# A selective scan that carries its state between chunks: GpSimd's additions to the first column against a first value read by the scan

## The chip, the core and the metric

The kernel runs on one core of a Trainium2 chip. The metric is the device time of one execution in microseconds, the median of several runs. All data are float32. The engines are PE (TensorE, matrix products), VectorE (DVE in the profile), ScalarE (ACT), GpSimd (POOL) and SyncE (SP), which issues nearly all DMAs.

## The reference

The program computes six layers on a tensor of 2 images of 64 x 64 positions with 128 channels: a convolutional selective scan (layer 0), a deformable convolution (layer 1), a selective scan (layer 2, first half), a spectral convolution (layer 2, second half), linear attention, and a mixture of experts. The change lies in the selective scan of layer 2:

```python
x_proj = x @ W_in
xs, z = jnp.split(x_proj, 2, axis=-1)
delta = xs @ W_delta
Bv = xs @ W_B
Cv = xs @ W_C
deltaA = jnp.exp(jnp.einsum('bld,dn->bldn', delta, A))
deltaB = jnp.einsum('bld,bln->bldn', delta, Bv)
def step(state, inp):
    dA_i, dB_i, x_i, C_i = inp
    state = dA_i * state + dB_i * x_i[:, None, :]
    y = jnp.einsum('bdn,bn->bd', state, C_i)
    return (state, y)
```

There are 2 images of 4096 tokens, 256 inner channels d and 256 state columns n. So for each image 256 x 256 first-order recurrences run over 4096 tokens.

## The kernel before, in words

`layer2` (L952 and following) runs the scan and, woven into it, the spectral convolution. Tokens are cut into chunks of T = 512: 8 chunks (c) for each of the 2 images (b), 16 chunks in all, in order. On the chip the 256 channels that the recurrence runs over independently are called d; the index n lies on the 128 partitions in two halves h.

For one chunk, d runs over 256 values, in 32 groups gi of DG = 8. Four values of d together are a row of work (R = 4); a chunk has 64 rows. For one row:

- SP loads `row` (L1306): delta for four d and 512 tokens, spread to all partitions (1 MB into SBUF). Three buffers; the load stands two rows ahead.
- GpSimd multiplies `row` by `g` into `S` (L1318), 128 x 4096 values: the inputs of the recurrences of four d and both halves. This stands one row ahead. `S` has three buffers of two rows.
- ScalarE makes `dA` = exp(delta x A) for one d and one h (L1374) into PSUM, three buffers.
- VectorE runs the recurrence over the 512 tokens of one d and one h in place in `S` (L1376, a scan: s[t] = dA[t] x s[t-1] + S[t]). Eight scans to a row.

After a group, `contract` lets PE multiply `S` with `cv` (L1336), ScalarE copies the product `ze` (L1342), and SP stores it.

Between the chunks of one image the last token's values must be carried over. ScalarE copies the last column of each group of `S` into the tile `state` (L1378), 128 partitions x 2 halves x 256 columns, in SBUF. In the next chunk of that image (c > 0) the kernel before forms the first step of the recurrence by hand. With delta of the first token, `scan_inputs` makes `ea` = exp(A x delta of the first token) (L909 to L914). GpSimd multiplies `state` by `ea`, most columns at d = 0 and the last 16 at d = 16 (L1323). After each multiplication L1318 it adds the decayed state to the first token's column of `S` (L1324, 128 x 8 values). The scan itself starts from the constant 0.

What goes beside the scan is written out by hand. `layer2` runs under a manual schedule: after each d the loop makes one step of each of several generators. These are `scan_inputs` for the next chunk (started at group 12 of 32), `outputs` for the chunk before, `contract`, and the spectral convolution (`convolve`, L1202, PE), which gets a share of steps by a credit. Each engine works its instructions in the order in which the loop records them. The inputs of the very first chunk are made during layer 1 by `first_inputs` and kept in DRAM.

Of the kernel before, what the change touches and what calls it, by code (L numbers as in the profile page):

```python
# [16 lines left out]
F32 = mybir.dt.float32  # L17
I32 = mybir.dt.int32
BF16 = mybir.dt.bfloat16
AF = mybir.ActivationFunctionType  # L20
ALU = mybir.AluOpType
# [4 lines left out]
P = 128  # L26
# [4 lines left out]
N = 512  # L31
# [835 lines left out]
    return (wdr, mdr), work  # L867


def scan_inputs(k, b, c, x1, rs, sh, w_in, a_t, sm, cst, gc, ddr, ps, got):  # L870

    nc, ins, T = k.nc, k.ins, N
    NB = T // P
    xi = sm.tile([P, NB, C], F32, name="xi", tag="s2")
    nc.sync.dma_start(out=xi, in_=x1[b * L + c * T : b * L + (c + 1) * T, :].rearrange("(i p) c -> p i c", p=P))
    for _ in range(4):
        yield
    pt = ps.tile([P, N], F32, name="pt", tag="ps")
    for j in range(NB):
        i = b * NTB + c * NB + j  # L880
        o = sm.tile([P, C], F32, name="xn", bufs=2)
        nc.scalar.activation(o, xi[:, j, :], AF.Identity, bias=sh[:, i : i + 1], scale=rs[:, i : i + 1])
        nc.tensor.transpose(pt[:, j * P : (j + 1) * P], o, k.ident)
        yield
    xt = sm.tile([P, T], F32, name="xt2", tag="s2")
    nc.scalar.copy(xt, pt)
    xtd = ddr.tile([P, T], F32, name="xtd")
    nc.sync.dma_start(out=xtd, in_=xt)
    yield
    xs = sm.tile([P, 2, N], F32, name="xs", tag="s4")  # L890
    for h in range(2):
        px = ps.tile([P, N], F32, name="px2", tag="ps")
        nc.tensor.matmul(px, w_in[:, h * P : (h + 1) * P], xt, start=True, stop=True)
        yield
        nc.scalar.copy(xs[:, h, :], px)
    ea = cst.tile([P, 2, 256], F32, name="ea")
    g = gc.tile([P, 2, T], F32, name="g")
    cv = gc.tile([P, 2, T], F32, name="cv")
    drow = ddr.tile([256, T], F32, name="drow")
    for w_, what in (("w_delta2", 0), ("w_b2", 1), ("w_c2", 2)):  # L900
        w = cst.tile([P, 2, 256], F32, name="w")
        nc.sync.dma_start(out=w, in_=ins[w_].rearrange("(a p) c -> p a c", p=P))
        yield
        yield
        if what == 0:

            pd = ps.tile([P, N], F32, name="pd0", tag="ps")
            for i in range(2):
                nc.tensor.matmul(pd[:, :256], xs[:, i, 0:1].to_broadcast([P, P]), w[:, i, :], start=i == 0, stop=i == 1)  # L909
            yield  # L910
            yield
            nc.vector.tensor_tensor(ea, a_t, pd[:, :256].unsqueeze(1).to_broadcast([P, 2, 256]), ALU.mult)
            yield
            nc.scalar.activation(ea, ea, AF.Exp)  # L914
        for h in range(2):
            pw = ps.tile([P, N], F32, name="pw2", tag="ps")
            for i in range(2):
                nc.tensor.matmul(pw, w[:, i, h * P : (h + 1) * P], xs[:, i, :], start=i == 0, stop=i == 1)
            yield
            yield  # L920
            if what == 0:
                d = sm.tile([P, N], F32, name="d", tag="s2")
                nc.scalar.copy(d, pw)
                nc.sync.dma_start(out=drow[h * P : (h + 1) * P, :], in_=d)
            elif what == 1:
                nc.vector.tensor_tensor(g[:, h, :], pw, xs[:, h, :], ALU.mult)
            else:
                nc.scalar.copy(cv[:, h, :], pw)
    got.append((xtd, g, cv, drow, ea))


def first_inputs(k, es, ps, dr, x1, rs, sh):

    nc = k.nc
    pool = es.enter_context(k.tc.tile_pool(name="l2e", bufs=1))
    w_in = pool.tile([P, 256], F32, name="w_in0")
    nc.sync.dma_start(out=w_in, in_=k.ins["w_in2"][:, :256])
    a_t = pool.tile([P, 2, 256], F32, name="a_t0")
    nc.sync.dma_start(out=a_t, in_=k.ins["a2"].rearrange("(a p) c -> p a c", p=P))
    got = []  # L940
    for _ in scan_inputs(k, 0, 0, x1, rs, sh, w_in, a_t, pool, pool, pool, dr, ps, got):
        pass
    xtd, g, cv, drow, ea = got[0]
    kept = []
    for t, name in ((g, "g0"), (cv, "cv0"), (ea, "ea0")):
        d = dr.tile(list(t.shape), F32, name=name)
        nc.sync.dma_start(out=d, in_=t)
        kept.append(d)
    return xtd, kept[0], kept[1], drow, kept[2]


def layer2(k, x1, x3, rs, sh, wdr, mdr, early):  # L952
# [13 lines left out]
    tc, nc, ins = k.tc, k.nc, k.ins  # L966
    T = N
    NB = T // P
    NCH = L // T
    DG = 8  # L970
    NG = 256 // DG
    R = 4
    HKW = 2 * (13 * P + DW)
    with ExitStack() as es:
# [34 lines left out]
            return x[t0 : t0 + T, :].rearrange("(i p) c -> p i c", p=P)  # L1009

        def prologue(b, c, got):
            return scan_inputs(k, b, c, x1, rs, sh, w_in, a_t, sm, cst, gc, ddr, ps, got)

        def epilogue(b, c, xtd, zd):

# [293 lines left out]
        def make_inputs(r):  # L1309
            i, r = divmod(r, 256 // R)  # L1310
            if i < len(todo):
                d = r * R
                gi, q = divmod(d, DG)
                if q == 0:
                    Ss[i, gi] = sp.tile([P, 2, DG, T], F32, name="S")
                S = Ss[i, gi][:, :, q : q + R, :]
                row, g, ea = rows[i, r], ready[i][1], ready[i][4]
                nc.gpsimd.tensor_tensor(S, row.unsqueeze(1).to_broadcast([P, 2, R, T]), g.unsqueeze(2).to_broadcast([P, 2, R, T]), ALU.mult)  # L1318
                if todo[i][1] > 0:
                    if d in (0, 2 * DG):  # L1320

                        m = slice(0, 256 - 2 * DG) if d == 0 else slice(256 - 2 * DG, 256)
                        nc.gpsimd.tensor_tensor(state[:, :, m], state[:, :, m], ea[:, :, m], ALU.mult)  # L1323
                    nc.gpsimd.tensor_tensor(S[:, :, :, 0], S[:, :, :, 0], state[:, :, d : d + R], ALU.add)  # L1324

        def contract(i, gi, zd):
            S, cv = Ss.pop((i, gi)), ready[i][2]
# [18 lines left out]

        with tc.manual_schedule():
            got = []
            xtd, g0, cv0, drow, ea0 = early
            g, cv, ea = gc.tile([P, 2, T], F32, name="g"), gc.tile([P, 2, T], F32, name="cv"), cst.tile([P, 2, 256], F32, name="ea")  # L1350
            for dst, src in ((g, g0), (cv, cv0), (ea, ea0)):
                nc.scalar.dma_start(out=dst, in_=src)
            ready[0] = xtd, g, cv, drow, ea
            for r in range(2):
                load_row(r)
            make_inputs(0)
            zq, save, credit = [], None, 0
            for i, (b, c) in enumerate(todo):
                _, g, cv, drow, ea = ready[i]
                zd = ddr.tile([NG, NB, P, 32, DG], F32, name="zd")  # L1360
                if i + 1 < len(todo):
                    pro = prologue(*todo[i + 1], got)
                for gi in range(NG):
                    for j in range(DG):
                        d = gi * DG + j
                        r = i * (256 // R) + d // R
                        if d % R == 0:
                            load_row(r + 2)
                            make_inputs(r + 1)
                        S = Ss[i, gi]  # L1370
                        row = rows[i, d // R]
                        for h in range(2):
                            dA = pa.tile([P, T], F32, name="dA2")
                            nc.scalar.activation(dA, row[:, j % R, :], AF.Exp, scale=a_t[:, h, d : d + 1])  # L1374
                            s = S[:, h, j, :]
                            nc.vector.tensor_tensor_scan(s, dA, s, 0.0, ALU.mult, ALU.add)  # L1376
                        if j == 2 and save is not None:
                            nc.scalar.copy(*save)  # L1378
                            save = None
                        advance(zq)  # L1380
                        if gi == 1 and j == 4 and i > 0:

                            side.append(outputs(*todo[i - 1], ready.pop(i - 1)[0], zd_))
                        if gi == 12 and j == 0 and i + 1 < len(todo):
                            side.append(pro)
                        step(side)
                        if got:
                            ready[i + 1] = got.pop()
                        now[0] += 1
                        credit = min(credit + 4.8, 4.8)  # L1390
                        credit -= spent[0]
                        spent[0] = 0
                        while credit > 0 and back:
                            credit -= step(back) or 4
                    if c < NCH - 1:
                        save = state[:, :, gi * DG : (gi + 1) * DG], S[:, :, :, T - 1]
                    zq.append(contract(i, gi, zd))
                zd_ = zd
# [367 lines left out]
```

## Time and profile before

| what | value |
|---|---|
| median of 3 runs | 15351.72 us (15348.02 to 15357.47) |
| the profiled execution's own time | 15384.23 us |
| its span, first to last instruction | 15382.4 us |
| layer 2's scans, first to last start | 5186.1 to 14882.6 us |
| busy: PE, DVE, ACT, POOL | 12387.6, 12707.2, 9497.0, 13019.5 us |
| L1324, GpSimd's addition to the first column | 896 times, 211 ns |
| L1323, GpSimd's decay of the state | 14 times 1212 ns, 14 times 257 ns |
| L912, VectorE, and L914, ScalarE, for `ea` | 16 times 660 ns, 16 times 630 ns |
| L1378, ScalarE's copy into `state` | 448 times, 202 ns |

The profile is one execution, so its times belong to that execution's 15384 us and not to the median. An engine's busy time counts its instructions, not its waits. A group of instructions is named by its line in the kernel, its engine, what it writes and reads, and its shape (partitions x elements). A wait is put down to the instruction that ended it. On VectorE the end of one instruction overlaps the start of the next in the records, so the distance between two starts says what an instruction costs there, and its duration says a little more.

### The profile page before, as it was taken

The page shows a single profiled execution, that of the slowest core. Times are in us where ns is not written, and L with a number is a line of the kernel's source. Part 1 is how long each engine was busy: PE and PEld are TensorE (multiplying, and loading weights), DVE is VectorE, ACT ScalarE, POOL GpSimd, SP SyncE. Part 2 cuts the span into 40 slices and gives each one's busy share as a digit, 9 for nine tenths or more (in the row PEclk, how much of TensorE's full clock was granted, in tenths as well). Part 3 has the DMA queues.
Part 4 walks back from the last instruction along what each step waited for, and adds up shares of the span by engine and source line. Part 5 has one row for each costly group of instructions (what it writes and reads, how often), then busy time and mean ns, then how long its engine had stood idle before and what let it go on. Part 6 is the DMA issues. An engine that isn't in the chain of part 4 may idle for free.

```text
span 15382.4 us, 234681 instructions
## 1 busy us (share of the span) xinstructions
PE 12387.6 (81%) x91214; PEld 7926.4 (52%) x91214; DVE 12707.2 (83%) x11405; ACT 9497.0 (62%) x14103; POOL 13019.5 (85%) x4168
## 2 busy tenths in 40 slices
PE   7888788888777545497896888978888899898897
PEld 4544454444577413254563555645445555555565
DVE  6777657777453799999999999999999999999973
ACT  4666436655001477777777677777777777777752
POOL 5888638888287899999999999999999999999960
PEclk8999899999888767698997999989999999999998
DMA  6888748888565445465555555555666666666543
GB/s 158 200 194 196 187 105 197 197 195 191 166 199 162 148 151 167 155 203 180 194 193 171 185 189 193 199 185 191 200 190 201 191 196 204 191 196 200 189 161 134
DMA packets 1444903, 2809.37 MB, mean 183 GB/s; under 512 B 393136, under 2 KB 1110608, under 8 KB 1240784
## 3 DMA queue, kind: packets, MB, share of 16 engines
q1 hardware_dynamic: 1395936, 2638.55, 58.3%
q0 software_dynamic: 46560, 153.18, 3.3%
q8 instruction: 721, 11.81, 0.3%
q14 instruction: 390, 3.19, 0.1%
q10 hardware_dynamic: 1296, 2.63, 0.0%
HBM read 2372.53 MB, written 421.31 MB: 182 GB/s over the span
## 4 chain that ended last, share of the span: by engine, by line
POOL 43%; PE 23%; DVE 12%; DMA 10%; issue 4%; ACT 3%; SPq 3%; another core or an unknown queue 1%; POOLq 0%; ACTq 0%; DVEq 0%
POOL S L1318 36%; DVE S L1376 9%; PE pef L1202 6%; DMA row<-drow 6%; POOL S L391 3%; PE Z L443 3%; PE Z L1336 2%; POOL G L742 2%; PE dA L411 2%; DMA W<-bcd 2%; PE acc L1175 2%; SPq L430 1%; DVE S L482 1%; PE pv L756 1%; PE pd L333 1%
## 5 line engine op out<-in xcount | busy, mean ns | idle before, releaser
L1376 DVE TENSOR_TENSOR_SCAN S<-dA,S 128x512 f32<-128x512 f32 x8192 | 9225.7, 1199 | 387.5 <-ACT dA L1374 204.1
L1318 POOL TENSOR_TENSOR S<-row,g 128x4096 f32<-128x4096 f32 x1024 | 9104.3, 8898 | 241.4 <-DMA row<-drow 159.7
L1374 ACT ACTIVATE dA<-row,a_t 128x512 f32<-128x512 f32 x8192 | 5614.6, 692 | 2165.9 <-DVE S L1376 2131.1
L1336 PE MATMUL Z<-S,cv 128*32 128x256 f32 x32768 | 2506.4, 436 | 1508.1 <-ACT ze L1342 1230.9
L1202 PE MATMUL pef<-hk,ur 128*128 128x256 f32 x14336 | 3514.1, 388 | 134.7 <-ACT e L1182 116.7
L1202 PEld LDWEIGHTS pef<-hk,ur 128*128 128x128 f32 x14336 | 2646.9, 191 | 1074.4 <-issue 564.1
L482 DVE TENSOR_TENSOR_SCAN S<-dA,S 128x1024 f32<-128x1024 f32 x1024 | 2309.3, 2283 | 758.6 <-ACT dA L425 422.8
L391 POOL TENSOR_TENSOR S<-row,bt 128x2048 f32<-128x2048 f32 x512 | 2383.8, 4656 | 432.8 <-PE Z L443 334.3
L1336 PEld LDWEIGHTS Z<-S,cv 128*32 128x32 f32 x32768 | 1003.4, 121 | 2718.1 <-issue 1229.5
L443 PE MATMUL Z<-S,W 128*32 128x128 f32 x16384 | 1191.5, 434 | 438.4 <-DMA W<-bcd 218.1
L1342 ACT COPY ze<-Z 128x512 f32<-128x512 f32 x1024 | 1122.4, 1096 | 232.5 <-PE Z L1336 196.2
L425 ACT ACTIVATE dA<-dA 128x1020 f32<-128x1020 f32 x1024 | 1028.6, 1010 | 378.0 <-PE dA L411 339.3
L411 PE MATMUL dA<-dt,quad 64*128 64x255 f32 x8192 | 1183.4, 414 | 19.8 <-DVE S L482 19.3
L443 PEld LDWEIGHTS Z<-S,W 128*32 128x32 f32 x16384 | 715.0, 170 | 818.3 <-issue 288.1
L1175 PE MATMUL acc<-e,mw 128*128 128x512 f32 x1920 | 1048.4, 634 | 29.6 <-ACT e L1182 28.8
L411 PEld LDWEIGHTS dA<-dt,quad 64*128 64x128 f32 x8192 | 750.9, 195 | 580.4 <-issue 385.3
L1202 PEld LDWEIGHTS pef<-hd,ur 128*128 128x128 f32 x4096 | 758.3, 194 | 493.7 <-issue 235.0
L742 POOL DMA_INDIRECT G<-table,idx x576 | 807.2, 1401 | 219.8 <-issue 167.9
L1202 PE MATMUL pef<-hd,ur 128*128 128x256 f32 (+1 forms) x4096 | 876.7, 340 | 102.0 <-ACT e L1182 95.5
L749 DVE TENSOR_TENSOR G<-G,wt 128x4608 f32<-128x4608 f32 x64 | 317.8, 4966 | 557.0 <-DMA G<-table,idx 537.2
L1182 ACT COPY e<-pef 128x512 f32<-128x512 f32 x960 | 557.9, 587 | 109.6 <-PE pef L1202 60.7
L756 PE MATMUL pv<-ident,G 128*128 128x128 f32 x4608 | 569.2, 285 | 30.0 <-issue 29.6
(341 smaller groups left out, 7858.9 us busy)
## 6 DMA issues: line engine op xcount, KB each, us to landing
row<-drow SPq DMA_DIRECT2D x1536, 1024.0 KB
zd<-ze SPq DMA_DIRECT2D x1024, 256.0 KB
hk<-in_phi_dram SPq DMA_DIRECT2D x128, 576.5 KB
hk<-in_phi_dram SPq DMA_DIRECT2D x96, 704.5 KB
hd<-in_phi_dram SPq DMA_DIRECT2D x512, 128.5 KB
mw<-wdr SPq DMA_DIRECT2D x480, 128.0 KB
hk<-in_phi_dram SPq DMA_DIRECT2D x160, 320.5 KB
hk<-in_phi_dram SPq DMA_DIRECT2D x96, 448.5 KB
```

The lines of the kernel that those rows point to most:

```text
L391: nc.gpsimd.tensor_tensor(S[:, o, :], rows.pop(s), bt[:, sub * T : (sub + 1) * T].unsqueeze(1).to_broadcast([P, 8, T]), ALU.mult)
L411: nc.tensor.matmul(dA[:, 2 * a + h, rest], stats[d, j][r, h, :], dt[r, h, at : at + T - 1], start=True, stop=True)
L443: nc.tensor.matmul(Z[32 * q : 32 * q + 32, :, :, a].rearrange("p t g -> p g t"), w, S[:, :, t : t + 13 : 4], start=True, stop=True)
L482: nc.vector.tensor_tensor_scan(flat, dflat, flat, 0.0, ALU.mult, ALU.add)
L742: nc.gpsimd.indirect_dma_start(out=G[:, o, :], out_offset=None, in_=table[b], in_offset=bass.IndirectOffsetOnAxis(ap=idxs[b][:, i * 9 + o ...
L1175: nc.tensor.matmul(acc.rearrange("p a s -> p (a s)"), ms[f][:, o, :], e, start=box["first"], stop="whole" in box and (f, o) == todo[-1])
L1202: nc.tensor.matmul(pe[:, a, 256 - n :], ur[:, par, j, :], h[:, at : at + n], start=i == 0, stop=i + 1 == len(mm))
L1318: nc.gpsimd.tensor_tensor(S, row.unsqueeze(1).to_broadcast([P, 2, R, T]), g.unsqueeze(2).to_broadcast([P, 2, R, T]), ALU.mult)
L1336: nc.tensor.matmul(Z[32 * j : 32 * j + 32, q], cv[:, h, s], S[:, h, :, s], start=h == 0, stop=h == 1)
L1342: nc.scalar.copy(ze.rearrange("p q t e -> p q e t"), Z)
L1374: nc.scalar.activation(dA, row[:, j % R, :], AF.Exp, scale=a_t[:, h, d : d + 1])
L1376: nc.vector.tensor_tensor_scan(s, dA, s, 0.0, ALU.mult, ALU.add)
```

## The change

Each scan of a chunk with c > 0 takes its first value from the column of `state` that belongs to its d and h, in place of the constant 0. With that, s[0] = dA[0] x state + S[0], and dA[0] is the same exponential that `ea` was. GpSimd's additions (L1324) and the decay of the state (L1323) go, and with them all that made `ea`: the two products, the multiplication and the exponential in `scan_inputs`, with three of the generator's steps, the load of `a2` into `a_t0`, and the store and load of `ea0` for the first chunk. ScalarE's copy into `state` stays as it is.

```diff
-def scan_inputs(k, b, c, x1, rs, sh, w_in, a_t, sm, cst, gc, ddr, ps, got):
+def scan_inputs(k, b, c, x1, rs, sh, w_in, sm, cst, gc, ddr, ps, got):
...
-    ea = cst.tile([P, 2, 256], F32, name="ea")
...
-        if what == 0:
-
-            pd = ps.tile([P, N], F32, name="pd0", tag="ps")
-            for i in range(2):
-                nc.tensor.matmul(pd[:, :256], xs[:, i, 0:1].to_broadcast([P, P]), w[:, i, :], start=i == 0, stop=i == 1)
-            yield
-            yield
-            nc.vector.tensor_tensor(ea, a_t, pd[:, :256].unsqueeze(1).to_broadcast([P, 2, 256]), ALU.mult)
-            yield
-            nc.scalar.activation(ea, ea, AF.Exp)
...
-    a_t = pool.tile([P, 2, 256], F32, name="a_t0")
-    nc.sync.dma_start(out=a_t, in_=k.ins["a2"].rearrange("(a p) c -> p a c", p=P))
...
-    for t, name in ((g, "g0"), (cv, "cv0"), (ea, "ea0")):
+    for t, name in ((g, "g0"), (cv, "cv0")):
...
-                row, g, ea = rows[i, r], ready[i][1], ready[i][4]
+                row, g = rows[i, r], ready[i][1]
                 nc.gpsimd.tensor_tensor(S, row.unsqueeze(1).to_broadcast([P, 2, R, T]), g.unsqueeze(2).to_broadcast([P, 2, R, T]), ALU.mult)
-                if todo[i][1] > 0:
-                    if d in (0, 2 * DG):
-
-                        m = slice(0, 256 - 2 * DG) if d == 0 else slice(256 - 2 * DG, 256)
-                        nc.gpsimd.tensor_tensor(state[:, :, m], state[:, :, m], ea[:, :, m], ALU.mult)
-                    nc.gpsimd.tensor_tensor(S[:, :, :, 0], S[:, :, :, 0], state[:, :, d : d + R], ALU.add)
...
-            for dst, src in ((g, g0), (cv, cv0), (ea, ea0)):
+            for dst, src in ((g, g0), (cv, cv0)):
                 nc.scalar.dma_start(out=dst, in_=src)
...
-                            nc.vector.tensor_tensor_scan(s, dA, s, 0.0, ALU.mult, ALU.add)
+                            nc.vector.tensor_tensor_scan(s, dA, s, state[:, h, d : d + 1] if c > 0 else 0.0, ALU.mult, ALU.add)
```

More of the change, by code (lines that the diff above doesn't have):

```diff
@@ L928, in scan_inputs @@
                 nc.scalar.copy(cv[:, h, :], pw)
-    got.append((xtd, g, cv, drow, ea))
+    got.append((xtd, g, cv, drow))
 def first_inputs(k, es, ps, dr, x1, rs, sh):
@@ L937, in first_inputs @@
     nc.sync.dma_start(out=w_in, in_=k.ins["w_in2"][:, :256])
-    a_t = pool.tile([P, 2, 256], F32, name="a_t0")
-    nc.sync.dma_start(out=a_t, in_=k.ins["a2"].rearrange("(a p) c -> p a c", p=P))
     got = []
-    for _ in scan_inputs(k, 0, 0, x1, rs, sh, w_in, a_t, pool, pool, pool, dr, ps, got):
+    for _ in scan_inputs(k, 0, 0, x1, rs, sh, w_in, pool, pool, pool, dr, ps, got):
         pass
-    xtd, g, cv, drow, ea = got[0]
+    xtd, g, cv, drow = got[0]
     kept = []
-    for t, name in ((g, "g0"), (cv, "cv0"), (ea, "ea0")):
+    for t, name in ((g, "g0"), (cv, "cv0")):
         d = dr.tile(list(t.shape), F32, name=name)
@@ L948, in first_inputs @@
         kept.append(d)
-    return xtd, kept[0], kept[1], drow, kept[2]
+    return xtd, kept[0], kept[1], drow
 def layer2(k, x1, x3, rs, sh, wdr, mdr, early):
@@ L1011, in prologue @@
         def prologue(b, c, got):
-            return scan_inputs(k, b, c, x1, rs, sh, w_in, a_t, sm, cst, gc, ddr, ps, got)
+            return scan_inputs(k, b, c, x1, rs, sh, w_in, sm, cst, gc, ddr, ps, got)
         def epilogue(b, c, xtd, zd):
@@ L1348, in layer2 @@
             got = []
-            xtd, g0, cv0, drow, ea0 = early
-            g, cv, ea = gc.tile([P, 2, T], F32, name="g"), gc.tile([P, 2, T], F32, name="cv"), cst.tile([P, 2, 256], F32, name="ea")
-            for dst, src in ((g, g0), (cv, cv0), (ea, ea0)):
+            xtd, g0, cv0, drow = early
+            g, cv = gc.tile([P, 2, T], F32, name="g"), gc.tile([P, 2, T], F32, name="cv")
+            for dst, src in ((g, g0), (cv, cv0)):
                 nc.scalar.dma_start(out=dst, in_=src)
-            ready[0] = xtd, g, cv, drow, ea
+            ready[0] = xtd, g, cv, drow
             for r in range(2):
@@ L1358, in layer2 @@
             for i, (b, c) in enumerate(todo):
-                _, g, cv, drow, ea = ready[i]
+                _, g, cv, drow = ready[i]
                 zd = ddr.tile([NG, NB, P, 32, DG], F32, name="zd")
```

## The prediction

> **What bounds the kernel now.** First the chain of work that ended last, on the page, with its costliest groups: the chain's shares by engine and by line, then line, engine, operation, count, busy time and mean ns of one, and the idle time before it.
>
> ```profile
> POOL 43%; PE 23%; DVE 12%; DMA 10%; issue 4%; ACT 3%; SPq 3%; another core or an unknown queue 1%; POOLq 0%; ACTq 0%; DVEq 0%
> POOL S L1318 36%; DVE S L1376 9%; PE pef L1202 6%; DMA row<-drow 6%; POOL S L391 3%; PE Z L443 3%; PE Z L1336 2%; POOL G L742 2%; PE dA L411 2%; DMA W<-bcd 2%; PE acc L1175 2%; SPq L430 1%; DVE S L482 1%; PE pv L756 1%; PE pd L333 1%
> ...
> L1376 DVE TENSOR_TENSOR_SCAN S<-dA,S 128x512 f32<-128x512 f32 x8192 | 9225.7, 1199 | 387.5 <-ACT dA L1374 204.1
> L1318 POOL TENSOR_TENSOR S<-row,g 128x4096 f32<-128x4096 f32 x1024 | 9104.3, 8898 | 241.4 <-DMA row<-drow 159.7
> ```
>
> GpSimd's multiplications lead the chain, but the 8192 scans of VectorE are as long in sum. So the second view is layer 2 cut into its chunks (chunks 0, 7, 8 and 9 of 16): length, then the busy time of PE, PEld, DVE, ACT and POOL.
>
> ```profile
> 5197.00:5770.00 573.00, 239.77 (x2052) 97.64 (x2052) 573.00 (x517) 414.73 (x619) 566.52 (x67) 0.62 0.41 149
> ...
> 9428.00:10030.00 602.00, 524.73 (x3694) 349.71 (x3692) 579.12 (x528) 433.26 (x641) 583.67 (x137) 0.95 0.58 195
> 10030.00:10628.00 598.00, 506.69 (x3562) 332.06 (x3562) 578.58 (x532) 433.90 (x664) 572.46 (x77) 0.92 0.60 194
> 10628.00:11233.00 605.00, 477.54 (x3303) 282.75 (x3303) 581.57 (x530) 463.79 (x736) 584.95 (x141) 0.94 0.62 192
> ```
>
> The additions under change exist only where c > 0, so chunks 0 and 8 already run without them. VectorE and GpSimd lie within 2% of each other everywhere: two engines share the bound. Third, the timeline of one row (four state columns, eight scans): start, duration, and for a merged line how many.
>
> ```profile
> 9002.94 8.92 POOL L1318 TENSOR_TENSOR S<-row,g 128x4096 f32<-128x4096 f32 x1
> 9011.93 0.21 POOL L1324 TENSOR_TENSOR S<-S,state 128x8 f32<-128x8 f32 x1
> 9012.10 8.92 POOL L1318 TENSOR_TENSOR S<-row,g 128x4096 f32<-128x4096 f32 x1
> ```
>
> ```profile
> 5299.81 100.39 DVE L1376 TENSOR_TENSOR_SCAN S<-dA,S 128x512 f32<-128x512 f32 x90
> ```
>
> GpSimd needs 9.16 us from row to row (9012.10 - 9002.94). VectorE, where nothing stops it (chunk 0), starts a scan every (100.39 - 1.20)/89 = 1.115 us, 8.92 us for a row. So with the addition GpSimd is late by 0.2 us a row; without it the two are equal. Last, for whom VectorE waits in layer 2 (us, times, longest):
>
> ```profile
> DVE S L1376 <- ACT dA L1374: 204.1, 145, 7.3
> ...
> DVE S L1376 <- POOL S L1324: 113.1, 82, 6.2
> ...
> DVE S L1376 <- POOL S L1318: 8.7, 3, 4.4
> ```
>
> Budget of the 9697 us from the first to the last scan's start (5186.1 to 14882.6): scans 8191 x 1.1145 = 9129; VectorE's other work about 75 (255 instructions of L926, L1040, L1077, L1063, L1264, L912 and the like, 92 busy, less about 0.08 overlap each); 490 left. Of it 204 + 122 are the waits above. The rest I share out as lateness that shows as no idle time, because a scan's start normally overlaps its predecessor by 0.08 us (1.199 - 1.115): about 100 to GpSimd (0.2 us in 896 rows is 180 in sum, so 220 for GpSimd is the right size), 20 to ScalarE, 45 to small issue gaps. So: GpSimd 220, ScalarE 225.
>
> **What is removed.** In 14 chunks x 64 rows, 896 additions (211 ns, 189 us) and 28 decays of the state (20.6 us) leave GpSimd. They lie on the chain, and with the gap around them they set the 9.16. GpSimd's row falls to about 8.95. Worth: the 220 us that VectorE loses to GpSimd, less what a late row transfer still costs (the multiplication waits 160 us for row<-drow). I take 200 regained.
>
> The 16 sums for ea go too: two PE products (L909), L912 on VectorE (0.66 us, 15 in layer 2: 9 us after overlap), L914 on ScalarE with its 23.6 us of waiting, a load of a2, a store and a load of ea on the DMA queues. The generator has three steps fewer, so its later parts move up by three of the 512 steps of a chunk; its result is needed only half a chunk later, so nothing waits for it. SP's queue loses two transfers and gains none. Only L912's 9 us lie on a bound engine; ScalarE's wait is counted below.
>
> **What is added.** 7168 scans (8 x 896) read their first value from a column of state, [128, 1] in SBUF, in place of the constant 0. The wait it brings costs nothing: ScalarE wrote that column (L1378) in the chunk before, some 600 us earlier, and the scan already waits for a later ScalarE instruction, its dA. In the built program these scans name the same engines as before, or fewer.
>
> The read itself is the disputed cost; no scan of this trace has one. The nearest rows are VectorE instructions with and without a per-partition scalar from SBUF:
>
> ```profile
> L1063 DVE SCALAR_TENSOR_TENSOR xo<-po,xo 128x256 f32<-128x256 f32 x32 | 12.8, 399 | 46.0 <-DMA xo<-x 46.0
> ...
> L541 DVE SCALAR_TENSOR_TENSOR Y<-U,dsum,py 128x256 f32<-128x256 f32 x64 | 29.4, 480 | 107.3 <-PE py L538 107.3
> ...
> L1508 DVE TENSOR_TENSOR lg<-G,lg 128x512 f32<-128x512 f32 x8 | 5.1, 682 | 0.0
> ...
> L1509 DVE SCALAR_TENSOR_TENSOR G<-ex,sm,lg 128x512 f32<-128x512 f32 x8 | 5.6, 744 | 0.0
> ...
> L1002 DVE COPY perm<-ident 128x64 f32<-128x64 f32 x2 | 17.3, 8695 | 2.9 <-DMA x<-X 2.9
> ```
>
> L1063 and L541 are one operation, one size, one tensor from PSUM and one from SBUF, as the scan has them; L1063's scalar is the constant 0.5, L541's is dsum in SBUF: 399 against 480, +81 ns. L1509 against L1508 gives +62, but across two operations. Could it hide in the overlap of neighbours? The timeline says no:
>
> ```profile
> 1957.83 1.12 DVE L574 SCALAR_TENSOR_TENSOR xr<-po,rs,xr 128x128 f32<-128x128 f32 x4
> ...
> 5821.80 0.40 DVE L1063 SCALAR_TENSOR_TENSOR xo<-po,xo 128x256 f32<-128x256 f32 x1
> 5822.12 3.44 DVE L1376 TENSOR_TENSOR_SCAN S<-dA,S 128x512 f32<-128x512 f32 x3
> ```
>
> L1063 frees the engine after 0.32 us, its duration less 0.08. L574, with a scalar from SBUF, starts every (1.12 - 0.342)/3 = 0.259 us, again its duration (342 ns in its row) less 0.083. The overlap is the same 0.08, so the scalar's time is added to every step. Bounds: 55 (the smallest difference of the starts around L1508 and L1509) to 83 ns. A gain is excluded: it is one operand more. I take 80, by the nearest row.
>
> [...]
>
> **Sum.** Scans 7168 x 0.080 = +573; L912 -9; waits for GpSimd -200; waits for ScalarE 225 -> 185, because a row then takes 8 x 1.195 = 9.56 us in place of 9.16 and ScalarE and PE have as much work as before, and L914's waits go: -40. Sum +324. The profiled execution took 15384.2 us (span 15382.4), 0.2% above the median of the runs, 15351.7; I add the difference to the median: **15676 us**. Everything outside layer 2 stays. What is late next: GpSimd no longer, with 0.6 us to spare a row; VectorE, and behind it ScalarE's dA.
>
> **The rivals.**
> - *The read hides* (faster). The next scan's scalar is fetched while the present scan still runs. [...] Against it: L574's and L541's steps. Then the row goes to 8.95 us: at most -200 - 9 - 40 = -249; at least what chunk 8 shows against 7 and 9, 598 against 603.5 (5.5 us x 14 = -77). Middle -165: 15187 us. It decides below (200 + 9 + 40)/7168 = 35 ns a scan; at 35 the change is worth nothing.
> - *The small price* (slower): 55 ns as around L1508. +394 - 9 - 200 - 40 = +145: 15497 us.
> [...]
> - *It does not do what it says*: excluded for the count, since the built program has no such additions left.
>
> **How the numbers follow.** Full price near 80 ns 0.69, small price 0.16, hidden read 0.10 (faster by over 0.2%), about 35 ns 0.03 (within 0.2%, about what a measurement of this kernel can tell from no change), lock 0.02. So faster 0.10, same 0.03, slower 0.87. Range: from 55 ns with the waits for ScalarE somewhat better (15490) to 83 ns with no wait for ScalarE gained and 175 from GpSimd, +595 - 9 - 175 = +411, 15763. The faster case and the lock stay outside.
>
> **What would show it.** Right: the scan's mean goes from 1199 to about 1280 ns in all but 1024 of them; VectorE's busy time rises by some 500 us; waits for S from GpSimd fall under 40 us; the chain goes from L1318 to the scan; GpSimd's idle time grows by 500 us and more. Chunks 0 and 8 keep 573 and about 598 us, the others go from 609 to about 631. Wrong: a scan's mean of 1199 (hidden), scans of several us beside L1318 (lock), or a PE that sets the chain.

## The result and the profile after

The changed kernel takes 15544.42 us (median of 4 runs, 15522.4 to 15560.52) against 15354.59 us before: 190 us more, a ratio of 1.0113 with a 95% interval of 1.0101 to 1.0125. The forecast was 15676 us, in a range of 15490 to 15763: slower, as forecast, and inside the range, but only 190 where the sum said 324.

The page of the changed kernel first: the chain's shares, then GpSimd's multiplications and the two kinds of scan (columns as before).

```profile
DVE 47%; PE 11%; POOL 3%; issue 3%; DMA 2%; ACT 1%; SPq 0%; ACTq 0%; DVEq 0%; POOLq 0%
...
L1305 POOL TENSOR_TENSOR S<-row,g 128x4096 f32<-128x4096 f32 x1024 | 9077.0, 8896 | 595.2 <-DMA row<-drow 476.9
L1357 DVE TENSOR_TENSOR_SCAN S<-dA,state,S 128x512 f32<-128x512 f32 x7168 | 8446.8, 1257 | 191.0 <-ACT dA L1355 149.4
...
L1357 DVE TENSOR_TENSOR_SCAN S<-dA,S 128x512 f32<-128x512 f32 x1024 | 1144.0, 1194 | 21.3 <-ACT dA L1355 15.2
```

The chain has gone from GpSimd (43%) to VectorE (47%). The last two rows are a control inside one program: same line, same shape, and the scans with a column of `state` take 1257 ns, those with a constant 1194. GpSimd now waits 477 us for its rows of delta, where it waited 160. That costs little, because GpSimd runs ahead: read from all rows with c > 0, its multiplication ends 4.2 us (median) before the row's first scan starts, where it ended 0.3 us before, with the addition still to come. VectorE's waits, for ScalarE and for GpSimd (us, times, longest):

```profile
DVE S L1357 <- ACT dA L1355: 164.6, 95, 5.5
...
DVE S L1357 <- POOL S L1305: 46.9, 28, 5.2
```

122 us of waiting for GpSimd have become 47, 204 for ScalarE have become 165. The step without stops, and chunks 0, 7, 8 and 9 (length, then busy PE, PEld, DVE, ACT, POOL):

```profile
8999.90 110.72 DVE L1357 TENSOR_TENSOR_SCAN S<-dA,state,S 128x512 f32<-128x512 f32 x94
```

```profile
5185.00:5760.00 575.00, 242.32 (x2048) 97.47 (x2048) 572.82 (x516) 413.70 (x618) 572.58 (x65) 0.62 0.41 149
9479.00:10101.00 622.00, 527.92 (x3684) 349.62 (x3684) 607.12 (x529) 436.87 (x643) 573.58 (x74) 0.95 0.57 188
10101.00:10696.00 595.00, 504.40 (x3555) 330.09 (x3556) 576.03 (x528) 431.70 (x660) 565.87 (x74) 0.92 0.60 194
10696.00:11323.00 627.00, 482.94 (x3303) 285.33 (x3301) 607.82 (x530) 468.62 (x735) 572.34 (x75) 0.93 0.59 186
```

A scan starts every (110.72 - 1.26)/93 = 1.177 us; read from all starts in the trace the median step is 1.175, against 1.1145 before. Chunks 0 and 8, in which nothing changed but the sums for `ea`, keep their length within 3 us (573 and 598 before). Chunks 7 and 9 grow by 20 and 22 us; by the scans' starts the 14 chunks with c > 0 grow from 609 to 622 us in the mean, so these two are more than typical. Over layer 2, the scans' starts span 9872 us against 9697: +175, as much as the two profiled executions differ (15558.7 against 15382.4 us of span). The loss lies wholly in the chunks with c > 0.

### The profile page after: what moved, and what is told of

It is laid out like the page before. It is cut to its first block, busy times and chain, and to the rows that moved or that the text cites. A ratio compares the mean times of both kernels' runs of the same rounds, so it can differ in the third digit from the quotient of the medians.

```text
span 15558.7 us, 233652 instructions
## 1 busy us (share of the span) xinstructions
PE 12417.1 (80%) x91150; PEld 7924.0 (51%) x91150; DVE 13054.2 (84%) x11389; ACT 9540.5 (61%) x14085; POOL 12824.6 (82%) x3244
## 4 chain that ended last, share of the span: by engine, by line
DVE 47%; PE 11%; POOL 3%; issue 3%; DMA 2%; ACT 1%; SPq 0%; ACTq 0%; DVEq 0%; POOLq 0%
DVE S L1357 46%; PE pef L1189 5%; POOL S L1305 3%; PE Z L1317 2%; PE acc L1162 1%; DMA row<-drow 1%; PE pw L907 1%; ACT ze L1323 1%; ACT dA L1355 0%; PE acc L1224 0%; DMA w<-in_w_delta_dram 0%; DMA w<-in_w_b_dram 0%; DMA e<-mdr 0%; PE pkv L1420 0%; PE pp L1497 0%
## 5 line engine op out<-in xcount | busy, mean ns | idle before, releaser
L1357 DVE TENSOR_TENSOR_SCAN S<-dA,state,S 128x512 f32<-128x512 f32 x7168 | 8446.8, 1257 | 191.0 <-ACT dA L1355 149.4
L1323 ACT COPY ze<-Z 128x512 f32<-128x512 f32 x1024 | 1120.6, 1094 | 220.6 <-PE Z L1317 214.7
L1357 DVE TENSOR_TENSOR_SCAN S<-dA,S 128x512 f32<-128x512 f32 x1024 | 1144.0, 1194 | 21.3 <-ACT dA L1355 15.2
```

The costliest lines, as they stand in the source:

```text
L1323: nc.scalar.copy(ze.rearrange("p q t e -> p q e t"), Z)
L1357: nc.vector.tensor_tensor_scan(s, dA, s, state[:, h, d : d + 1] if c > 0 else 0.0, ALU.mult, ALU.add)
```

## The experiments

Two questions were open after the result. Why was an operand that should cost 80 ns worth 61? And how do its price and the gain on GpSimd combine? Theory A: a row takes as long as the longer of two engines, so a price on one and a gain on the other do not add. Rival B: they add. The kernels of one group ran on the same chip with the kernel before, whose median was 15353.99 us for the first four and 15351.6 for the last two.

**The scalar alone.** GpSimd's work stays; only the scan's operand changes.

```diff
+        zcol = cst.tile([P, 1], F32, name="zcol")
+        nc.vector.memset(zcol, 0.0)
...
-                            nc.vector.tensor_tensor_scan(s, dA, s, 0.0, ALU.mult, ALU.add)
+                            nc.vector.tensor_tensor_scan(s, dA, s, zcol if c > 0 else 0.0, ALU.mult, ALU.add)
```

> The kernel before with one edit: the scans of the chunks with c > 0 take their first value from a column of zeros in SBUF instead of the constant 0. All of GpSimd's work stays. Theory A (the longer of two engines): a scan's step goes from 1.115 to 1.175 us, so a row takes 9.40 us on VectorE against 9.15 on GpSimd, and GpSimd's additions are hidden behind it. The time is then that of the changed kernel or up to 40 us more: 15545 to 15590 us. Rival B (price and gain are independent terms): 7168 x 0.061 = +434 us over the kernel before, 15790 us. Both expect a mean of about 1257 ns for a scan; a mean near 1199 would say that it is not the operand at all that made the scans longer.

Measured: 15551.32 us, ratio 1.0128 (1.0113 to 1.0144), +197 us. Its page, and GpSimd's timeline in it:

```profile
L1378 DVE TENSOR_TENSOR_SCAN S<-dA,zcol,S 128x512 f32<-128x512 f32 x7168 | 8450.5, 1256 | 182.3 <-ACT dA L1376 122.6
```

```profile
9000.92 8.90 POOL L1320 TENSOR_TENSOR S<-row,g 128x4096 f32<-128x4096 f32 x1
9009.89 0.21 POOL L1326 TENSOR_TENSOR S<-S,state 128x8 f32<-128x8 f32 x1
9010.05 8.89 POOL L1320 TENSOR_TENSOR S<-row,g 128x4096 f32<-128x4096 f32 x1
```

GpSimd still adds in every row and needs 9.13 us (9010.05 - 9000.92), and the time is that of the changed kernel within 7 us. So the 896 additions are hidden once a row takes 9.40 us on VectorE. Theory A holds; rival B is off by 240 us. Of the 434 us that the operand costs VectorE, 197 show: the rest fills time that VectorE had lost anyway.

**The removal alone.** The changed kernel, with the constant 0 back.

```diff
-                            nc.vector.tensor_tensor_scan(s, dA, s, state[:, h, d : d + 1] if c > 0 else 0.0, ALU.mult, ALU.add)
+                            nc.vector.tensor_tensor_scan(s, dA, s, 0.0, ALU.mult, ALU.add)
```

> The changed kernel with one edit: every scan starts from the constant 0. So GpSimd's additions and decays are gone and no scan reads a column; the state is not carried from chunk to chunk, which leaves out a part of the computation. Theory A: VectorE's row is 8.92 us, GpSimd's about 8.95, and the two can no longer hide each other's delays: between -77 us (what chunk 8 showed against its neighbours) and -200 us against the kernel before, 15155 to 15280 us. Rival C (the additions were hidden anyway, so the whole change is the price of the operand less a few side effects): within 30 us of the kernel before, 15325 to 15385 us.

Measured: 15230.4 us, ratio 0.9915 (0.9901 to 0.9928), -124 us. So the removed part is worth something, and rival C falls. It is worth less than the 200 us that the prediction took. The waits of this kernel's VectorE show what is left:

```profile
DVE S L1357 <- ACT dA L1355: 235.6, 147, 7.6
DVE S L1357 <- POOL S L1305: 85.4, 50, 6.5
```

The 122 us of waiting for GpSimd have become 85, where the changed kernel has 47, and the 204 for ScalarE have become 236. GpSimd's row takes 8.86 us here (the median step of its multiplications), VectorE's 8.92, so GpSimd can make up only 0.06 us a row after a late one; in the changed kernel it is about 0.5. That this margin makes the difference fits the waits; no run separates it.

The two parts alone give +197 and -124, in sum +73; together they give +190. The difference is the gain that the longer scans made worthless.

**Every second row.** The scan reads the column in half of the rows, GpSimd adds in the other half. In the kernel before:

```diff
+                        st_, ea_ = (t[:, :, m].rearrange("p h (g e) -> p h g e", e=DG)[:, :, :, 0:R] for t in (state, ea))
-                        nc.gpsimd.tensor_tensor(state[:, :, m], state[:, :, m], ea[:, :, m], ALU.mult)
+                        nc.gpsimd.tensor_tensor(st_, st_, ea_, ALU.mult)
+                    if q == 0:
...
-                            nc.vector.tensor_tensor_scan(s, dA, s, 0.0, ALU.mult, ALU.add)
+                            nc.vector.tensor_tensor_scan(s, dA, s, state[:, h, d : d + 1] if c > 0 and j >= R else 0.0, ALU.mult, ALU.add)
```

> The kernel before, but in every second row (the upper four columns of each group of eight) the scans read the column of state, and GpSimd adds and decays only for the other rows. Theory A: two rows take 8.92 + 9.40 = 18.32 us on VectorE and 2 x 8.95 + 0.2 = 18.1 on GpSimd; before it was 18.3 on GpSimd. So the time stays at that of the kernel before, or up to 40 us above it: 15350 to 15395 us. Rival B (each row costs what it costs in the changed kernel, or before): half of the change's +190, 15450 us.

Measured: 15371.51 us, ratio 1.0011 (1.0002 to 1.002), +18 us. Half of the edit costs a tenth of the whole, not a half: theory A.

**A scalar in another operation.** This one asks why 80 was wrong.

```diff
+        cols = cst.tile([P, 2], F32, name="cols")
...
-                nc.vector.scalar_tensor_tensor(zt, zt, 1.0, pg, ALU.add, ALU.mult)
+                nc.vector.scalar_tensor_tensor(zt, zt, cols[:, 0:1], pg, ALU.add, ALU.mult)
...
-                nc.vector.scalar_tensor_tensor(o, po[:, : 2 * P].rearrange("p (a c) -> p a c", c=C), 0.5, o, ALU.mult, ALU.add)
+                nc.vector.scalar_tensor_tensor(o, po[:, : 2 * P].rearrange("p (a c) -> p a c", c=C), cols[:, 1:2], o, ALU.mult, ALU.add)
```

> The kernel before, with the constants 1.0 of L1040 and 0.5 of L1063 put into SBUF columns: 32 + 32 instructions that had a constant read a per-partition scalar, and nothing else differs. Theory D (a scalar from SBUF costs some 61 ns in any operation, and the pair L1063 and L541 of the prediction differed by 20 ns for another reason): L1063 goes from 399 to about 460 ns, L1040 from 661 to about 722. Rival E (this operation pays 81 ns, a scan less): about 480 and 742 ns. The time stays within 20 us of the kernel before under both.

Measured (one run, 15362.06 us): L1040 and L1063 stand three lines lower here.

```profile
L1043 DVE SCALAR_TENSOR_TENSOR zt<-zt,cols,pg 128x512 f32<-128x512 f32 x32 | 23.1, 722 | 37.0 <-ACT zt L1041 37.0
...
L1066 DVE SCALAR_TENSOR_TENSOR xo<-po,cols,xo 128x256 f32<-128x256 f32 x32 | 14.7, 458 | 45.2 <-DMA xo<-x 45.2
```

Before, the means of the 32 were 662 and 399 ns: 60 and 59 ns more, in another operation and at two sizes. Theory D. L541, at 480, is then some 20 ns longer than L1066 for a reason of its own, and the trace of before already had one. There L1040 stands 30 times directly behind a scan, with no wait, and twice after the last of the scans, behind waits of over 18 us; the same operation on its own in that last stretch (count, then min, median and max ns):

```profile
L1040 DVE SCALAR_TENSOR_TENSOR zt<-zt,pg x2: 686/688/689, 14902.2 to 14946.0; 128x512 f32<-128x512 f32 x2
```

688 ns there, 661 between scans, with the same constant. L1063 goes from 397 to 424 likewise. L926 of the same trace tells the place and the wait apart. It stands 30 times between two scans, 7 of them behind a wait for PE (start, duration, and in brackets the idle time before):

```profile
6647.68 0.69 DVE L926 TENSOR_TENSOR g<-pw,xs 128x512 f32<-128x512 f32 x1 [0.33 <-PE pw L918]
6648.29 2.33 DVE L1376 TENSOR_TENSOR_SCAN S<-dA,S 128x512 f32<-128x512 f32 x2
...
6655.62 0.67 DVE L926 TENSOR_TENSOR g<-pw,xs 128x512 f32<-128x512 f32 x1
6656.20 4.56 DVE L1376 TENSOR_TENSOR_SCAN S<-dA,S 128x512 f32<-128x512 f32 x4
```

Behind a wait it takes 692 ns (median of the 7), directly behind a scan 666 (the 23 others), and the next scan starts 0.61 us after it against 0.58. The scans say the same: of those that follow a scan, the 739 that started over 60 ns late took 1223 to 1225 ns, the 6376 that started on time 1196 (median). So the 26 ns go with the wait and not with the place, and VectorE loses them. L541 began behind a wait in 30 of 64 cases (481 ns, about 475 in the others, none of which follows a scan). With L1066 behind a wait:

```profile
L1066 DVE SCALAR_TENSOR_TENSOR xo<-po,cols,xo x2: 483/484/485, 14904.0 to 14945.8; 128x256 f32<-128x256 f32 x2
```

All three behind a wait: 484 and 481 with a scalar from SBUF (L1066, L541), 424 with the constant (L1063). So the pair that I compared differed in two things, the scalar (about 60 ns) and what stood before the instruction (about 20).

**Every third row.** If the longer engine decides, the best split is where both are equally long. The decay is again confined to the columns that GpSimd adds.

```diff
+        def by_scan(d):
+            return d < 240 and d // R % 3 == 2
...
+                    if not by_scan(d):
                         nc.gpsimd.tensor_tensor(S[:, :, :, 0], S[:, :, :, 0], state[:, :, d : d + R], ALU.add)
...
-                            nc.vector.tensor_tensor_scan(s, dA, s, 0.0, ALU.mult, ALU.add)
+                            nc.vector.tensor_tensor_scan(s, dA, s, state[:, h, d : d + 1] if c > 0 and by_scan(d) else 0.0, ALU.mult, ALU.add)
```

> The kernel before, but in every third row (20 of the 64 of a chunk with c > 0) the scans read the column of state, and GpSimd adds and decays only for the other 44. Theory A (the longer of two engines), with the measured step of 1.175 us: over a chunk VectorE's row is 8.92 + 0.48 x 20/64 = 9.07 us, GpSimd's 8.95 + 0.2 x 44/64 = 9.09, against 9.15 before. So 0.06 x 896 = 54 us less at best, and since the two are then nearly equal, delays of one reach the other: 15300 to 15345 us. Rival B (rows cost what they cost in the two kernels, so a third of the change's +190): 15410 us.

Measured: 15334.96 us, ratio 0.9986 (0.9977 to 0.9995), -17 us. It is below both kernels, as theory A said, and rival B's sign is wrong. The gain is small, with an interval of 8 to 35 us. Only a third of the 54 us is there: VectorE still waits 84 us for GpSimd, which fits two level engines that wait for each other's delays, but no run separates that.

```profile
DVE S L1381 <- POOL S L1329: 73.0, 46, 5.2
DVE S L1381 <- POOL S L1321: 11.5, 7, 4.5
```

**The addition twice.** The last one asks what an addition costs where GpSimd is the longer engine.

```diff
+        zadd = cst.tile([P, 2, 4], F32, name="zadd")
+        nc.vector.memset(zadd, 0.0)
...
                     nc.gpsimd.tensor_tensor(S[:, :, :, 0], S[:, :, :, 0], state[:, :, d : d + R], ALU.add)
+                    nc.gpsimd.tensor_tensor(S[:, :, :, 0], S[:, :, :, 0], zadd, ALU.add)
```

> The kernel before with one instruction more in each row of the chunks with c > 0: GpSimd adds a tile of zeros to the first column, the same shape as its addition of the state. Scans start from the constant 0. Theory A: GpSimd's row goes from 9.15 to about 9.35 us, and it is the longer one, so the whole 0.2 x 896 = 180 us shows: 15520 to 15540 us. Rival F (an addition is worth what its removal gave, 124 us, since part of it lies hidden): 15480 us or less.

Measured: 15569.76 us, ratio 1.014 (1.0125 to 1.0156), +218 us. GpSimd's timeline, and whom VectorE waits for:

```profile
9000.17 8.91 POOL L1320 TENSOR_TENSOR S<-row,g 128x4096 f32<-128x4096 f32 x1
9009.15 0.21 POOL L1326 TENSOR_TENSOR S<-S,state 128x8 f32<-128x8 f32 x1
9009.44 0.21 POOL L1327 TENSOR_TENSOR S<-S,zadd 128x8 f32<-128x8 f32 x1
9009.60 8.91 POOL L1320 TENSOR_TENSOR S<-row,g 128x4096 f32<-128x4096 f32 x1
```

```profile
DVE S L1379 <- POOL S L1327: 350.4, 658, 6.6
```

The row takes 9.43 us (9009.60 - 9000.17), 0.28 more than before by the medians of all rows with c > 0. The second addition starts 0.29 us after the first: 0.21 us of work, and 0.08 between the end of one and the start of the other. 896 x 0.28 = 251 us; 218 show, 30 more than theory A's range allowed. So rival F falls and theory A's mechanism holds, but its price of 0.2 us was too small; where the other 33 us are is not shown. The first addition costs the same. Without one, in the changed kernel, GpSimd's timeline reads:

```profile
8996.33 70.92 POOL L1305 TENSOR_TENSOR S<-row,g 128x4096 f32<-128x4096 f32 x8
```

That is (70.92 - 8.90)/7 = 8.86 us a row, not the 8.95 of the prediction and the expectations, and 0.28 under the 9.14 of the kernel before (medians). In the first experiment, GpSimd's addition of the state was free.

## Why the prediction was right, and what was mis-sized

- **What bounds it**: right. Two engines within 2%, and the longer one decides; the scalar alone and the addition twice show it from both sides, and the two split kernels fit it.
- **The read of the column**: the direction was right (no hiding in the overlap), the size was not. "I take 80, by the nearest row" is the term that failed: 61 measured (a step of 1.175 us less 1.1145, from all starts), so 7168 x 0.0605 = 434 us in place of 573. The choice of the pair failed, as the scalar in another operation shows. The pair dismissed for crossing two operations, L1509 against L1508, both away from the scans, said 62; its starts say 61 where they are read to the nanosecond (662 against 601), and the 55 came from times rounded to 0.01 us.
- **GpSimd's waits**: -200 forecast. If every start of an instruction on VectorE that comes over 15 ns late is put down to what ended the wait, the lateness behind GpSimd fell from 229 to 50 us: -179. Of the 47 us of recorded waits that stay, about 32 stand behind rows of delta that landed late for GpSimd itself. GpSimd's own row was mis-sized (8.86 in place of 8.95, an addition at 0.28 in place of 0.2); it costs nothing here, since VectorE's 9.40 is longer than either.
- **ScalarE's waits**: -40 forecast, 220 to 176 by the same count, -45 before rounding.
- **L912**: -9 forecast, -9 measured. Two terms were missing. The instruction that begins behind a wait takes some 25 ns more, so the one after it starts late: 22 us before, 4 now, -18. And waits for PE fell from 18 to 10 us, -8.
- **The sum** by these: 434 - 179 - 45 - 9 - 18 - 8 = +175, the difference of the two spans of scans. With 0.0605 in place of 0.080, the prediction's own sum would have been 434 - 9 - 200 - 40 = +185, 15537 us, within 8 of the measured time. Some of that is luck: 21 us too many for GpSimd stand against 26 that were left out.
- **The signs**: the chain moved to the scan, and chunks 0 and 8 kept their length. The sizes that hang on the 80 ns missed: a scan's mean of 1257 ns (1280 forecast), VectorE's busy time up by 347 us (500), GpSimd's idle time by 371 us (500 and more). Waits for GpSimd fell to 47 us, not under 40.
- **The rivals**: the hidden read fell (1194 against 1257 ns in one program). The small price came nearest: its 55 ns was 6 too low, and its 15497 us lay 47 us under the measured time, where the forecast lay 132 above it. The lock, in which a scan that reads a column and GpSimd's multiplication run one after the other, fell: no scan took more than 1285 ns beside multiplications of 8.9 us, so a scan that reads a column is not held up behind one, as the copy L1002 was (8549 and 8841 ns for 64 elements, each copy ending 0.05 us after a multiplication). In all, the scalar adds 59 to 63 ns to each instruction here (59 for L1063, 60 for L1040, 63 between the two kinds of scan).

What stays open is why a wait makes the next instruction on VectorE some 26 ns longer, and why one directly behind a scan is shorter still than one directly behind another instruction (L926: 666 ns against 681 and 683, two cases).

## What to carry to other kernels

Where two engines are level, work taken off one is worth only as much as the other leaves, and of a price on the other only what goes beyond its slack shows: 124 us gained alone, 197 us of a price of 434 lost alone, 190 lost together. Multiply a per-instruction price by its count before moving work: one addition, 0.28 us of GpSimd's time for eight columns, was exchanged for eight times 60 ns of VectorE's. And price an operand from rows that differ in nothing else, a wait before them included; if one group's min and max lie apart, look at what stood before each of them.

## What the runs showed of the hardware

- A [128, 1] scalar from SBUF in place of a constant costs VectorE about 60 ns for each instruction, in the scan (1.1145 to 1.175 us a step) and in scalar_tensor_tensor (60 and 59 ns in the means), at 512 and at 256 elements, and the overlap with the next instruction does not hide it: in scalar_tensor_tensor the step to the next start grows by 61 and 60 ns too (579 to 640, 316 to 376, medians between scans).
- A VectorE instruction that begins behind a wait takes some 26 ns longer than the same one directly behind a scan (a product 692 against 666 ns, a scan 1224 against 1196), and the next one starts later by as much (608 against 582 ns after that product's start).
- A small addition on GpSimd (128x8) costs 0.28 us a row, the first (8.86 to 9.14 us) as well as a second (to 9.43), not the 0.21 us of its work.
